# A 0/1 matrix kept in DRAM as bytes in place of bfloat16, converted by the transfer that stores it

## The chip, the cores and the metric

The kernel runs on one NeuronCore of a Trainium2 chip. The metric is device microseconds (us) of one execution, and the time of a kernel is the median over its runs. Engines are called by their short names: PE (TensorE, matrix products and transposes), DVE (VectorE), ACT (ScalarE), POOL (GpSimd, which also issues indirect transfers and converting transfers), SP (SyncE, which issues most plain transfers). 16 DMA engines move the data of all queues.

## The reference

Four graph layers with a residual are applied one after the other to `x` (8 batches, 2048 nodes, 64 features). All use one matrix `adj` of 2048 x 2048, whose entries are 0 or 1 with ones on the diagonal, dense in its first rows and columns and sparse elsewhere.

```python
# layer 0
h = jnp.maximum(_layernorm(x), 0.0); x = x + _L0_gnn_ref(h, H, adj, ...)     # hypergraph attention, adj / deg
# layer 1
h = jnp.maximum(_layernorm(x), 0.0); x = x + _L1_gnn_ref(h, adj, ...)        # Chebyshev terms of adj
# layer 2: three steps of message passing
h = jnp.maximum(_layernorm(x), 0.0); v = h with node 0 set
for _ in range(3):
    effects = einsum('nm,bmd->bnd', adj, v)
    v = relu(concat([v, effects]) @ W1.T + b1) @ W2.T + b2
x = x + v
# layer 3: attention over adj (diagonal set to 1)
h = jnp.maximum(_layernorm(x), 0.0)
e = leaky_relu(e_src[:, :, None] + e_dst[:, None, :], 0.2)
x = x + softmax(adj * e) @ (h @ weight) + bias
```

In layer 3 a node needs, one by one, only the nodes that it is linked to. So the kernel wants for each node a short list of its neighbours' numbers.

## The kernel before

Nodes are cut into 16 blocks of 128 (`P`), features into 4 groups `q` of 128 rows that hold two batches each. The program checks the data first and then branches (`tile_gnn_stack_kernel`): with sparse 0/1 data it runs `layer0_pairs`, `layer1_near`, `layer2_near` and `layer3_near`; otherwise dense versions of them. The engines meet at the branch, so the start stage ends as a whole. The trace is of the sparse branch. Each stage writes its loops in Python; a scheduler in the build puts the instructions into a fixed order on each engine, and inserts the waits. An engine runs its instructions in that order.

**The start stage** (`start`, `check_adj`). For each of the 16 blocks t, SP loads 128 rows of `adj` as float32 (1 MB, L371) into one of four row buffers. ACT squares them into bfloat16 (`squares`, four buffers, L372) and sums the degree; DVE compares row and square (L373), which proves that all entries are 0 or 1; POOL clears the diagonal (L376) and stores the squared rows into the DRAM tensor `links` (L380). PE multiplies the block with a vector of ones to find the empty tiles (`seen`). Between these, the same stage normalises `x` in four chunks of 512 nodes and makes the first features: PE, ACT and DVE share their order with that work. DVE writes the flag for the branch at its end (L639).

**Layer 2** (`layer2_near`). Three steps go over the 16 blocks. In a step, an object `Feed` brings the rows of the last step's messages from the DRAM tensor `sent`, for block 0 by plain transfers of SP (L2576), for the others by indirect gathers of POOL (L2578); six `raw` buffers are in flight. ACT rounds each raw tile (`part_hi`, L2595), DVE makes the remainder (`part_lo`, L2596), PE adds both products into the accumulator `acc`. DVE adds a block's own term and writes the finished tile `z` (L2639), PE transposes it (`pz`, L1918), ACT applies the relu (L1920), PE forms the next message `pn`, DVE adds a constant and writes `u` (L1872), which SP stores to `sent` (L1876). Up to two blocks are late behind the one that is gathered.

**The neighbour lists** (`neighbours`) are made beside steps 0 and 1 of layer 2: the generator is advanced by one piece after each group of gathered tiles, and step 2 opens with what is left of it. It ranks the nodes by degree (`order`); then, for each of the blocks 1 to 15 of that order, POOL gathers the 128 rows of `links` (L1999), DVE multiplies them with the line 1, 2, 3, ... in float16 (L2003), so that a row holds the numbers of its neighbours, and takes the eight largest (L2009) as often as the block's longest list needs, erasing them in between (L2012). The list lands in `near` (L2016), which layer 3 uses. The rows lie in two buffers, the products in two others; both are views of the slot `q4` of 16 KB per partition:

```python
words = slots.tile([P, 2, N], F, name="near_rows", tag="q4")
rows = words[:, 0].bitcast(BF).rearrange("p (i n) -> p i n", i=2)
named = words[:, 1].bitcast(F16).rearrange("p (i n) -> p i n", i=2)
```

The trace calls the slots `q`, so L2003 appears there as `q<-q,q`.

Of the kernel before, what the change touches and what calls it, by code (L numbers as in the profile page):

```python
# [8 lines left out]
BF = mybir.dt.bfloat16  # L9
# [12 lines left out]
N = 2048  # L22
# [31 lines left out]
class Slots:  # L54
# [3 lines left out]
    def __init__(self, pool):  # L58
        self.flat = {f"q{i}": pool.tile([P, 2 * N], F, name=f"q{i}") for i in range(6)}
        self.pool = None  # L60
# [74 lines left out]
class Kernel:  # L135
# [8 lines left out]
    def __init__(self, tc, ctx, a):  # L144
        self.tc, self.nc, self.a = tc, tc.nc, a
        self.flip = 0
        self.short = False
        self.consts = ctx.enter_context(tc.tile_pool(reuse_waits="tile", name="consts", bufs=1))

        dram = ctx.enter_context(tc.tile_pool(reuse_waits="tile", name="dram", bufs=1, space=bass.MemoryType.DRAM))  # L150
        self.xs = [
            [a["xT"][:, :, c * CW : (c + 1) * CW].rearrange("q p n -> p q n") for c in range(NC)]
        ]


        self.h_rows = dram.tile([N, ROW], F, name="h_rows")
        self.g_rows = dram.tile([N, NB * D], F, name="g_rows")
        self.order3 = dram.tile([P, 2, NT], I32, name="order3")

        self.links = dram.tile([N, N], BF, name="links")  # L160
        self.sent = [dram.tile([N, NB * D], F, name=f"sent{i}") for i in range(5)]


        self.f_rows = dram.tile([N, WIDE], F, name="f_rows")
        self.att_rows = dram.tile([N, NB * D], F, name="att_rows")
        self.rdeg = dram.tile([NT, P], F, name="rdeg")

        self.h_sums = [dram.tile([8, P, CW], F, name=f"sums{q}") for q in range(NP)]
        self.h_parts = [dram.tile([P, 3, N], BF, name=f"parts{q}") for q in range(NP)]
        for i in range(3):  # L170
            self.xs.append([dram.tile([P, NP, CW], F, name=f"x{i}_{c}") for c in range(NC)])
        self.setup()
# [1802 lines left out]
    def neighbours(self, k, bank, slots):  # L1975

        nc = self.nc
        order = k.tile([P, 2, NT], I32, name="order")  # L1980
        w = Parts(slots.tile([P, 2 * N], F, name="sort", tag="q4"))
        rank = self.ranks(w, bank, 1, NEAR[1])
        yield
        self.by_rank(w, bank, rank, order)
        nc.sync.dma_start(self.order3, order)
        yield
        near = self.near
        words = slots.tile([P, 2, N], F, name="near_rows", tag="q4")
        rows = words[:, 0].bitcast(BF).rearrange("p (i n) -> p i n", i=2)
        named = words[:, 1].bitcast(F16).rearrange("p (i n) -> p i n", i=2)  # L1990
        words = slots.tile([P, 2, N], F, name="line", tag="q5")
        whole = words[:, 0].bitcast(I32)
        line = words[:, 1, : N // 2].bitcast(F16)
        nc.gpsimd.iota(whole, pattern=[[1, N]], base=1, channel_multiplier=0)
        nc.vector.tensor_copy(line, whole)
        yield
        for t in range(1, NT):
            raw, row = rows[:, t % 2], named[:, t % 2]
            nc.gpsimd.indirect_dma_start(  # L1999
                raw, None, self.links[:],  # L2000
                bass.IndirectOffsetOnAxis(ap=order[:, 1, t : t + 1], axis=0),
            )
            nc.vector.tensor_mul(row, raw, line)  # L2003
            yield
            most = -(-NEAR[t] // 8)
            top = k.tile([P, 24], F, name="top", bufs=2)
            for i in range(most):
                eight = top[:, 8 * i : 8 * i + 8]
                nc.vector.max(out=eight, in_=row)  # L2009
                yield  # L2010
                if i + 1 < most:
                    nc.vector.match_replace(  # L2012
                        out=row, in_to_replace=eight, in_values=row, imm_value=0.0
                    )
                    yield
            nc.vector.tensor_copy(near[:, FIRST[t] : FIRST[t + 1]], top[:, : NEAR[t]])  # L2016
# [1113 lines left out]
```

## Time and profile before

| | |
|---|---|
| median of 4 runs | 2032.41 us (2028.54 to 2039.38) |
| the profiled execution | 2035.78 us, its span 2034.0 us |
| mean granted clock of PE | 0.902 of full speed |
| busy shares of the span | PE 84%, DVE 69%, POOL 51%, ACT 40% |
| DMA, mean over the span | 305.20 MB, 150 GB/s |
| L380, stores of `links` | 16 of 512 KB, issued from 20.5 to 90.9 us |
| L1999, gathers of `links` | 15, issued from 1326.2 to 1536.8 us |
| L2003, multiplications | 15, 1217 ns mean |

A span is the time between the first and the last instruction that the profiler sees; the execution's own time has a little around it. All places below are in us from the start of the span. A line of a timeline gives start, duration, engine, line of the kernel, instruction, what it writes and reads; in square brackets stands how long the engine was idle before it and what ended that. A wait line gives the total, how often, and the longest.

### The profile page before, as it was taken

Reading aid. Unit: us, or ns where it says so; the run is one execution under the profiler, and the core shown is the slowest. Engines: PE = TensorE matmul, PEld = TensorE weight load, DVE = VectorE, ACT = ScalarE, POOL = GpSimd, SP = SyncE. Lnnn points to the kernel's source line nnn. Section 1 sums busy time; section 2 is a strip of 40 time slices with the busy share of each in tenths; the row PEclk is TensorE's granted clock in tenths of the full one; section 3 lists DMA queues with packets and bytes.
Section 4 is the critical chain, followed back from the end, with each engine's and each line's share of the span. In section 5 each row is a group of like instructions: output and inputs, shape, how many; then the busy total and the mean of one; then the engine's idle time right before and its main releaser. Section 6 shows DMA issues by size and latency. Waiting matters only on the chain. (4 is left out here: it accounts for less than half of the span.)

```text
span 2034.0 us, 22332 instructions
## 1 busy us (share of the span) xinstructions
PE 1717.2 (84%) x7061; PEld 977.8 (48%) x7066; DVE 1411.4 (69%) x2389; ACT 808.7 (40%) x1627; POOL 1038.7 (51%) x959
## 2 busy tenths in 40 slices
PE   6859899999896778999999998779788898578885
PEld 2425766665224444443443343557566564334432
DVE  6778778884576666776767556688787566357874
ACT  5712344554555653222110100455556553166400
POOL 1100166676861644876655545364564531557870
PEclk8867899998887888999999999789899899678997
DMA  9640223334326774232230211577677664746655
GB/s 345 245 117 1 82 77 102 110 125 162 118 73 206 227 243 141 78 100 82 71 91 25 83 51 43 180 216 253 215 237 254 203 209 151 243 137 172 174 171 190
DMA packets 124057, 305.20 MB, mean 150 GB/s; under 512 B 29312, under 2 KB 31120, under 8 KB 118160
## 3 DMA queue, kind: packets, MB, share of 16 engines
q0 software_dynamic: 45328, 149.60, 24.2%
q1 hardware_dynamic: 76288, 149.80, 21.9%
q10 hardware_dynamic: 2304, 4.20, 0.6%
q8 instruction: 59, 0.97, 0.2%
q14 instruction: 78, 0.64, 0.1%
HBM read 240.40 MB, written 63.14 MB: 149 GB/s over the span
## 5 line engine op out<-in xcount | busy, mean ns | idle before, releaser
L2578 POOL DMA_INDIRECT raw<-sent,index x300 | 316.8, 1056 | 339.4 <-DVE part_lo L2596 139.8
L2596 DVE TENSOR_TENSOR part_lo<-raw,part_hi 128x512 fp32r<-128x512 f32 x352 | 265.2, 777 | 134.0 <-ACT part_hi L2595 83.2
L2595 ACT CAST part_hi<-raw 128x512 fp32r<-128x512 f32 x352 | 210.8, 619 | 312.2 <-PE acc L176 223.5
L1840 POOL TENSOR_TENSOR half<-half,y 128x512 f32<-128x512 f32 x192 | 247.1, 1316 | 134.2 <-DVE y L1834 129.0
L176 PE MATMUL pk<-q,w 128*128 128x512 f32 (+1 forms) x768 | 302.0, 610 | 2.3 <-DVE q L1724 0.9
L176 PE MATMUL acc<-q,ident 128*128 128x512 f32 x416 | 206.0, 619 | 42.8 <-issue 23.8
L176 PE MATMUL acc<-part_hi,weights 128*128 128x512 f32 x365 | 176.4, 486 | 31.6 <-ACT part_hi L2595 21.3
L176 PE MATMUL acc<-part_lo,weights 128*128 128x512 f32 x365 | 169.4, 466 | 38.0 <-DVE part_lo L2596 25.2
L1834 DVE SCALAR_TENSOR_TENSOR y<-pk,bias,q 128x512 f32<-128x512 f32 x224 | 158.0, 743 | 52.1 <-PE pk L176 32.9
L176 PEld LDWEIGHTS pk<-q,w 128*128 128x128 f32 (+1 forms) x768 | 116.0, 190 | 156.2 <-issue 120.9
L2819 POOL DMA_INDIRECT ring<-f_rows,near x121 | 142.2, 1176 | 71.8 <-issue 31.3
L176 PEld LDWEIGHTS acc<-q,ident 128*128 128x128 f32 x416 | 77.1, 196 | 120.8 <-issue 74.1
L176 PEld LDWEIGHTS acc<-part_lo,weights 128*128 128x128 f32 x365 | 74.5, 204 | 92.1 <-DVE part_lo L2596 50.9
L2305 POOL TENSOR_TENSOR q<-q,beta 128x512 f32<-128x512 f32 x57 | 76.0, 1336 | 72.5 <-DVE beta L2281 33.8
L176 PEld LDWEIGHTS acc<-part_hi,weights 128*128 128x128 f32 x365 | 74.4, 204 | 78.9 <-issue 41.2
L176 PE MATMUL pp<-adj,x_ind_hi 128*128 128x512 f32 x256 | 89.4, 465 | 0.5 <-DVE q L846 0.3
L2890 DVE TENSOR_TENSOR q<-ring,e 128x1024 f32<-128x1024 f32 x58 | 70.0, 1218 | 22.1 <-remote 17.3
L2564 ACT CAST hub_weights<-dense 128x384 fp32r<-128x384 bf16 x80 | 40.6, 512 | 109.2 <-PE acc L176 101.6
L2305 POOL TENSOR_TENSOR q<-q,coef 128x512 f32<-128x512 f32 x57 | 63.0, 1106 | 21.0 <-DVE q L2328 17.6
L176 PE MATMUL pp<-adj,x_ind_lo 128*128 128x512 f32 x256 | 72.7, 403 | 0.0
L287 DVE RECIPROCAL std<-std 128x512 f32<-128x512 f32 x16 | 53.6, 3351 | 26.8 <-ACT std L286 26.8
L2489 POOL DMA_INDIRECT listed_raw<-in_adjT_dram,cell x60 | 63.2, 1053 | 16.5 <-issue 16.1
(503 smaller groups left out, 3443.7 us busy)
## 6 DMA issues: line engine op xcount, KB each, us to landing
rows<-in_adj_dram SPq DMA_DIRECT2D x16, 1024.0 KB
adj_t<-in_adjT_dram SPq DMA_DIRECT2D x64, 256.0 KB
own<-sent SPq DMA_DIRECT2D x52, 256.0 KB
raw<-sent SPq DMA_DIRECT2D x52, 256.0 KB
sent<-u SPq DMA_DIRECT2D x48, 256.0 KB
q<-x SPq DMA_DIRECT2D x10, 1024.0 KB
x<-q SPq DMA_DIRECT2D x9, 1024.0 KB
links<-squares POOLq DMA_DIRECT2D x16, 512.0 KB
```

Of the source, the lines that this page charges most:

```text
L176: self.nc.tensor.matmul(out, lhsT, rhs, start=start, stop=stop)
L287: nc.vector.reciprocal(std, std)
L1834: nc.vector.scalar_tensor_tensor(y, pks[b, half], bias[:, b : b + 1], emb[:, b], op0=OP.add, op1=OP.mult,)
L1840: add.tensor_add(acc, acc, y)
L2305: self.nc.gpsimd.tensor_tensor(x, x, by.unsqueeze(2).to_broadcast([P, NB, D]), op=OP.mult)
L2489: self.kern.behind(nc.gpsimd.indirect_dma_start(raw[:, i], None, rows, bass.IndirectOffsetOnAxis(ap=self.cell[:, c + i : c + i + 1], axis= ...
L2564: self.nc.scalar.copy(to, self.lists.dense[:, :, i * P : (i + 1) * P])
L2578: self.nc.gpsimd.indirect_dma_start(raw, None, self.rows[:], bass.IndirectOffsetOnAxis(ap=self.lists.index[:, c : c + 1], axis=0),)
L2595: nc.scalar.copy(hi, raw)
L2596: nc.vector.tensor_sub(lo, raw, hi.bitcast(F))
L2819: self.nc.gpsimd.indirect_dma_start(to, None, self.kern.f_rows[:], bass.IndirectOffsetOnAxis(ap=index, axis=0))
L2890: nc.vector.tensor_tensor(y.rearrange("n i (b f) -> n i b f", b=NB), block[:, i : i + 2, : NB * D].rearrange("n i (b f) -> n i b f", b=NB) ...
```

## The change

`links` becomes a tensor of unsigned bytes. The store at L380 reads bfloat16 from SBUF and writes bytes, so the transfer converts; its text is the same as before. A gather at L1999 brings 2 KB per row in place of 4 KB, into the lower half of the old place; the multiplication at L2003 reads bytes and a float16 line, and writes float16 as before.

```diff
-        self.links = dram.tile([N, N], BF, name="links")
+        self.links = dram.tile([N, N], mybir.dt.uint8, name="links")
...
-        rows = words[:, 0].bitcast(BF).rearrange("p (i n) -> p i n", i=2)
+        rows = words[:, 0, : N // 2].bitcast(mybir.dt.uint8).rearrange("p (i n) -> p i n", i=2)
```

The scheduler gives the same order as before outside layer 2. Within it, some instructions trade places with near neighbours on PE, ACT, DVE, POOL and SP.

## The prediction

> **What bounds the kernel now.** I first asked where the links are touched: the groups and the instructions of the tile links. There are two places: 16 stores (L380, 20.5 to 90.9 us) and 15 gathers (L1999, 1326 to 1537 us) with a multiplication behind each (L2003). I then read each place in its own stage, since the chain that ended last begins only at 1597 us. The busy times by stretch, for layer 2 while the rows are sorted into lists (after the length of a stretch come PE, PEld, DVE, ACT and POOL busy with their instructions, then granted clock, DMA share, GB/s):
>
> ```profile
> core 0: us, PE busy (x) PEld busy (x) DVE busy (x) ACT busy (x) POOL busy (x), PEclk, DMA share, GB/s
> 1330.00:1440.00 110.00, 91.44 (x489) 71.68 (x490) 100.25 (x124) 61.82 (x124) 56.80 (x51) 0.91 0.75 237
> 1440.00:1478.00 38.00, 27.39 (x114) 20.22 (x113) 23.48 (x30) 20.11 (x40) 26.42 (x25) 0.82 0.66 204
> 1478.00:1560.00 82.00, 71.63 (x422) 60.40 (x423) 69.54 (x95) 45.43 (x95) 41.89 (x40) 0.96 0.80 256
> ```
>
> DVE is busy for 91% of the first stretch and is the limit; in the second it has 14.5 us of slack; in the third PE (87%) and DVE (85%) wait for each other. The DVE groups of 1320 to 1560 us (busy, mean ns, then idle time before):
>
> ```profile
> L2009 DVE MAX8 top<-q 128x8 f32<-128x2048 f16 x21 | 48.0, 2286 | 0.0
> L2003 DVE TENSOR_TENSOR q<-q,q 128x2048 f16<-128x2048 bf16 x15 | 18.3, 1217 | 0.0
> ```
>
> Both read 2048 elements per partition. L2003, whose three operands are all of 16 bits, takes little over half as long as MAX8. In the start stage, the three-operand row over 2048 elements with float32 among its inputs is as slow as MAX8:
>
> ```profile
> L373 DVE SCALAR_TENSOR_TENSOR equal<-rows,squares 128x2048 bf16<-128x2048 f32 x16 | 36.7, 2293 | 5.0 <-ACT squares L372 4.8
> ```
>
> Next, DVE in order of time, to see what stands behind a multiplication:
>
> ```profile
> 1397.53 1.88 DVE L2596 TENSOR_TENSOR part_lo<-raw,part_hi 128x512 fp32r<-128x512 f32 x3
> 1399.34 0.17 DVE L2016 COPY near<-top 128x12 f32<-128x12 f32 x1
> 1399.43 1.21 DVE L2003 TENSOR_TENSOR q<-q,q 128x2048 f16<-128x2048 bf16 x1
> 1400.56 0.73 DVE L2639 SCALAR_TENSOR_TENSOR z<-own,self_weight,acc 128x512 f32<-128x512 f32 x1
> ```
>
> z, the finished tile of the step, starts the moment L2003 is done. PE transposes it at 1401.65 (L1918), 0.36 us after z is ready at 1401.29. So L2003 has 0.36 us to spare here.
>
> The start stage is the other place. Between 10 and 80 us the DMA engines are 98% busy. What of that reaches the path is read from ACT's waits of 10 to 100 us, and from ACT in order of time:
>
> ```profile
> ACT squares L372 <- DMA rows<-in_adj_dram: 8.7, 3, 5.1
> ACT squares L372 <- POOL squares L376: 2.0, 2, 1.7
> ```
>
> ```profile
> 43.38 1.91 ACT L372 ACTIVATE squares<-rows 128x2048 bf16<-128x2048 f32 x1 [5.13 <-DMA rows<-in_adj_dram]
> ```
>
> One wait is large: row block 6 arrives 5.13 us late, and ACT's copies for the layer normalisation stand behind it. The queues of 10 to 100 us (packets, MB, share of 16 engines):
>
> ```profile
> q1 hardware_dynamic: 6886, 19.41, 59.3%
> q0 software_dynamic: 2304, 8.39, 23.0%
> ```
>
> **The change part by part.**
>
> *The multiplication, L2003.* Its first operand becomes bytes. No row here shows an operand of 8 bits. Bounds: 1.22 us (nothing lost) and 2.29 us (the rows of 2048 elements at one element per step). I take 2.29: the only rows near 1.2 us for two sources have all operands of 16 bits. That is +1.07 us, 15 times, 16.0 us of DVE. The Trainium skill, "VectorE: DVE Perf Modes", section "What auto-detection actually checks", says that two elements per cycle from packing need every tensor of the instruction to be 16-bit; its table for 2048 elements gives about 1224 and 2293 ns for two speeds and one, and the first agrees with the 1217 ns measured here. By that rule the bytes cost what I took from MAX8; by the hopeful end of the rows they would cost nothing.
>
> How much of the 16.0 us reaches the end I work out for each multiplication:
> - Five at 1331 to 1421 us, in the stretch that DVE limits. Behind the first DVE has no idle time until the second. For the other four the spare time between the end of the z behind them and its transposition on PE is 0 (PE had already waited 2.84 us for z), 0.05, 0.36 and 0.22 us. Delay: 5 x 1.07 - 0.63 = 4.7 us.
> - Three at 1440, 1455 and 1467 us. The next idle times of DVE behind them are 2.06, 3.89 and 2.17 us, and POOL issues its gathers there nearly back to back. Cover: those idle times, which end with data from POOL's gathers or from ACT. If it failed, because a later part_lo frees POOL's buffers later, it would cost 3.2 us. I take 1.0.
> - Seven at 1478 to 1553 us. z is transposed 0.06, 0.06, 0.23, 0.06, 0.27, 0.89 and 0.59 us after its end; the start costs of PE make the 0.06 nothing to spare. Delay: 7 x 1.07 - 0.23 - 0.27 - 0.89 - 0.59 = 5.5 us.
>
> Together 11.2 us, with ends of 0 (all of it swallowed by other waits of PE) and 16.0. Behind L2003 on DVE are queued z, u and the part_lo of the next tile; PE waits for z and part_lo, POOL's gathers for the buffers that part_lo frees. Steps 0 and 1 pass the delay on whole: step 2 opens only when all lists are done.
>
> *The 15 gathers, L1999.* POOL still issues 15 instructions of 0.94 us for 128 rows each; each row is 2 KB in place of 4 KB, so 3.9 of the 36.2 MB of the software queue between 1320 and 1560 us go. ACT's part_hi waits 13.7 us for raw gathers from that queue; 11% of it is 1.5 us, and not all lies on the path. I take -1.0 us, ends 0 and -3.
>
> *The 16 stores, L380.* The issue on POOL is 0.55 us and POOL is idle for 71 us before its affine selects; a dearer issue is covered by that. The transfer reads 4 KB per partition as before and writes 2 KB. 23.0% of 90 us is 20.7 us with all 16 engines, 1.3 us a store. No transfer here converts. Bounds from this row: priced by the bytes written, it halves; with the conversion as a second pass, it doubles. Four stores (blocks 0 to 3) are issued before the late block 6 lands, 5.2 us of engine time: -2.6 us or +5.2 us at that wait. Over all 16 stores it is -10.3 or +20.7 us of engine time, of which the hopeful side finds only the 8.7 + 2.0 us of waits above, and the DVE order (57 of 70 us busy) behind them. I take 0, the middle of two bounds without a row to choose by, because the side that is read keeps its rows of 4 KB and the engines' time is what is full; the queues ran at 23 and 25 GB/s an engine while they were (19.41 MB in 59.3%, 8.39 MB in 23.0%, of 16 engines for 90 us). The Trainium skill, "DMA: Bandwidth & Descriptors", section "Anatomy of one DMA", prices a transfer at about 2.0 us plus its bytes over 436 GB/s, and does not say which side's bytes count when the two differ; by the written side its estimate is 0.6 us less a store.
>
> *Order.* The order of the instructions differs only in layer 2: one gather of links is issued one raw gather earlier, one multiplication stands before a u and not behind it, a few sent stores trade places with raw loads on SP's queue, and on PE the hub products and part products interleave differently. Nothing crosses a step. I price it at 0, ends -3 and +3, about half of the time from one z to the next (z starts at 1384.0, 1391.0, 1396.3 and 1400.6 us). No buffer and no wait is added.
>
> **Sum.** 4.7 + 1.0 + 5.5 - 1.0 + 0 + 0 = +10.2 us. The profiled execution took 2035.78 us (span 2034.0); with the change it would be 2046.0. It lies 3.4 us above the median of the runs, 2032.41, so the median becomes 2042.6 us. The likeliest case's own range, with 5 to 16.0 us for L2003 and the rest as above, is 2036 to 2047.
>
> **The rivals.**
>
> *The conversion is dear.* If a store keeps its engines twice as long, block 6 comes 5.2 us later, blocks 8 to 11 find four more stores ahead, and ACT's reuse of the four squares buffers, which already waits for the store of block 7 (issued 51.8 us, free at 61.4), waits for longer. Some 10 to 20 us on top of layer 2: 2053 to 2063. For it: DMA 98% busy for 70 us, and stores are a quarter of it. Against it: the packets read stay the same.
>
> *Not slower: layer 2 swallows the multiplications.* In the third stretch PE is idle for 10.4 us and ACT waits 18.5 us for PE. If the delayed z only eats idle time that PE has anyway, less than 4 us of the 11.2 stay; with 1.5 us from the gathers and 2.6 us at block 6 the total is about zero: 2030 to 2036. It decides if the z behind L2003 is late by less than the next wait of PE for something else, tile by tile. Against it: 91% DVE in the first stretch, whose 4.7 us have nowhere to go.
>
> *The bytes don't slow DVE.* L2003 stays at 1.22 us; -1 us from the gathers is left: about 2031.
>
> **How the numbers follow.** Forecast 0.54, half of it on each side of +0.5% (2042.6); dear conversion 0.22; swallowed 0.18; bytes free 0.06. 0.5% or 10 us is about what a measurement of this kernel can tell from no change; the four runs span 2028.5 to 2039.4. Slower by more: 0.27 + 0.21 = 0.48. Within: 0.27 + 0.20 of the other three = 0.47. Faster: 0.05, where a cheaper store lets the whole start stage shrink. The range reaches down to 2031, which holds the swallowed case but for its lower part, and up to 2057, which holds the lower part of the dear one.
>
> **What would show it.** L2003 at about 2290 ns; DVE busy up by 16 us in 1330 to 1560 and the end of step 1 (last L2003 at 1552.6) later by 10 us than the start of that stage; the z to pz spare times gone. The start: flag (L639), at 106.4 us now, within 2 us. I am wrong if L2003 stays at 1.2 us, if flag moves by over 5 us, or if q0's share in 10 to 100 us leaves 23% by more than a quarter.

## The result, and the profile after

| | before | after |
|---|---|---|
| median | 2034.97 us (78 runs, 2022.99 to 2050.15) | 2037.38 us (52 runs, 2025.05 to 2053.76) |
| ratio, 95% interval | | 1.0016 [1.0004, 1.0029] |

The change costs 3.3 us by the ratio (0.8 to 5.9): less than the bound of 0.5% and a third of the +10.2 us of the sum. On another chip, in the first experiment, the same kernel stood at 0.9983 [0.9964, 1.0001]. The two intervals just don't meet, so the cost isn't the same on every chip, or is known less well than one interval says.

The lines of after come from an execution of 2029.89 us (span 2028.1) of the first experiment, on a chip where the kernel before takes 2025.46 us, because the first profiled one (2061.30 us) lies above all 52 timed ones, with most of its surplus behind layer 2. The nodes are ranked (L539) 6 us earlier in it than in the profile of before, so the three stretches are moved by 6 us (columns as before):

```profile
core 0: us, PE busy (x) PEld busy (x) DVE busy (x) ACT busy (x) POOL busy (x), PEclk, DMA share, GB/s
1324.00:1434.00 110.00, 90.21 (x483) 69.73 (x484) 102.90 (x122) 61.92 (x124) 59.65 (x53) 0.92 0.73 224
1434.00:1472.00 38.00, 28.37 (x119) 21.29 (x118) 28.52 (x33) 20.93 (x41) 27.22 (x24) 0.78 0.61 178
1472.00:1554.00 82.00, 72.72 (x405) 59.19 (x405) 74.74 (x89) 47.45 (x95) 49.63 (x42) 0.92 0.75 233
```

DVE has 2.6, 5.0 and 5.2 us more in the three. PE's busy time hardly moves (191.3 in all, 190.5 before), and POOL's grows by 11.4 us, which no part of the sum had. The DVE groups of layer 2:

```profile
L2009 DVE MAX8 top<-q 128x8 f32<-128x2048 f16 x21 | 48.0, 2287 | 0.0
L2003 DVE TENSOR_TENSOR q<-q,q 128x2048 f16<-128x2048 uint8 x15 | 34.3, 2287 | 0.0
```

The multiplication runs at the speed of MAX8: 34.3 us in place of 18.3, the 16.0 us of the sum.

The multiplication that had 0.36 us to spare, in order of time over all engines (in brackets the idle time before, and what ended it):

```profile
1395.43 1.29 DVE L2596 TENSOR_TENSOR part_lo<-raw,part_hi 128x512 fp32r<-128x512 f32 x2
...
1396.64 0.18 DVE L2016 COPY near<-top 128x12 f32<-128x12 f32 x1
...
1396.73 2.28 DVE L2003 TENSOR_TENSOR q<-q,q 128x2048 f16<-128x2048 uint8 x1
...
1398.93 0.73 DVE L2639 SCALAR_TENSOR_TENSOR z<-own,self_weight,acc 128x512 f32<-128x512 f32 x1
...
1399.72 0.42 PEld L1918 LDWEIGHTS pz<-ident,z 128*128 128x128 f32 x4 [0.56 <-DVE z L2639]
```

This tile is as the forecast saw it: of the 1.07 us, the spare 0.36 are gone, and PE's weight load now waits 0.56 us for z. The question is why fifteen such delays don't add up to 11 us.

In the start, ACT's waits of 10 to 100 us, its late block 6, and the queues (packets, MB, share of 16 engines):

```profile
ACT squares L372 <- DMA rows<-in_adj_dram: 9.3, 4, 4.7
...
ACT squares L372 <- DMA links<-squares: 2.0, 2, 1.2
```

```profile
43.12 1.91 ACT L372 ACTIVATE squares<-rows 128x2048 bf16<-128x2048 f32 x1 [4.74 <-DMA rows<-in_adj_dram]
```

```profile
q1 hardware_dynamic: 6922, 19.41, 60.2%
q0 software_dynamic: 2304, 4.20, 25.1%
```

Half the bytes are written, in as many packets, and the engines are held a little longer, not shorter: 25.1% against 23.0%. Block 6 is 4.74 us late (5.13 before), and the flag (L639) comes at 107.8 us (106.4).

### The profile page after: what moved, and what is told of

It reads as the page before. It is cut to its first block, busy times and chain, and to the rows that moved or that the text cites. A ratio compares the mean times of both kernels' runs of the same rounds, so it can differ in the third digit from the quotient of the medians.

```text
span 2059.5 us, 22328 instructions
## 1 busy us (share of the span) xinstructions
PE 1730.2 (84%) x7061; PEld 983.7 (48%) x7066; DVE 1425.1 (69%) x2389; ACT 810.0 (39%) x1627; POOL 1048.9 (51%) x959
## 3 DMA queue, kind: packets, MB, share of 16 engines
q0 software_dynamic: 44368, 141.47, 23.7%
## 4 chain that ended last, share of the span: by engine, by line
PE 47%; DVE 13%; issue 9%; DMA 7%; POOL 6%; ACT 2%; another core or an unknown queue 2%; SPq 0%; POOLq 0%; DVEq 0%; ACTq 0%
PE pk L176 18%; PE acc L176 16%; POOL q L2305 3%; PE bank L176 3%; DMA raw<-sent,index 2%; PE p L176 2%; POOL raw L2578 1%; DVE q L2320 1%; PE pd L176 1%; DVE part_lo L2596 1%; PE pz L1918 1%; PE pn L176 1%; POOL ring L2819 1%; PE first L176 1%
## 5 line engine op out<-in xcount | busy, mean ns | idle before, releaser
L2578 POOL DMA_INDIRECT raw<-sent,index x300 | 329.9, 1100 | 334.0 <-DVE part_lo L2596 128.1
L176 PE MATMUL acc<-q,ident 128*128 128x512 f32 x416 | 214.0, 640 | 48.4 <-issue 20.1
L2890 DVE TENSOR_TENSOR q<-ring,e 128x1024 f32<-128x1024 f32 x58 | 69.9, 1217 | 26.3 <-remote 14.6
```

What stands on the lines that cost most here:

```text
L176: self.nc.tensor.matmul(out, lhsT, rhs, start=start, stop=stop)
L2578: self.nc.gpsimd.indirect_dma_start(raw, None, self.rows[:], bass.IndirectOffsetOnAxis(ap=self.lists.index[:, c : c + 1], axis=0),)
L2890: nc.vector.tensor_tensor(y.rearrange("n i (b f) -> n i b f", b=NB), block[:, i : i + 2, : NB * D].rearrange("n i (b f) -> n i b f", b=NB) ...
```

## The experiments

Besides the times I use one stretch of each profile: **steps 0 and 1 of layer 2**, from the order of the nodes (L539) to the end of the last z of step 1. It took 230.2 us before and 233.8 us in the profile shown above (236.2 in the first one of after). A single execution scatters by some 7 us to either side as a whole, so one such number is weak by itself.

### Which half costs: one part of the change at a time

These ran beside one another on one chip (before: 2025.46 us). **Again**, the changed kernel as it is:

> The changed kernel once more, for a second profile. Theory A (the multiplication's 16 us of DVE reach the end in part, the converting stores cost nothing): about 3 us over before, flag (L639) within 1 us of 106.4, and the last multiplication (L2003) 3 to 6 us later relative to flag. Theory B (DVE's time is swallowed altogether, the converting stores lengthen the start): flag 1.5 to 3 us later, the distance from flag to the last L2003 unchanged. The first profile had flag at 108.1 us and the last L2003 at 1557.8, against 106.4 and 1552.6 of before.

Measured: 2023.54 us, ratio 0.9983 [0.9964, 1.0001]; steps 0 and 1 in 233.8 us.

**16-bit integers**: the store converts as in the change, but nothing gets smaller and the multiplication keeps 16-bit operands. In the gathered rows, `BF` becomes `uint16` too.

```diff
-        self.links = dram.tile([N, N], BF, name="links")
+        self.links = dram.tile([N, N], mybir.dt.uint16, name="links")
```

> links kept as 16-bit unsigned integers: the store still converts, but every transfer has the bytes of before, and all operands of L2003 have 16 bits. Order as before on all engines. Theory A: L2003 stays at 1217 ns, time within 2 us of before. Theory B: 2 to 4 us slower, all of it before flag. q0 between 10 and 100 us: 23% if converting costs the engines nothing, 25% or more if it does.

Measured: 2030.19 us, 1.0007 [0.9978, 1.0037]; 232.1 us.

**A float32 line**: the kernel before with only L2003 slow.

```diff
-        line = words[:, 1, : N // 2].bitcast(F16)
+        line = words[:, 1]
```

> before, with the line of numbers in float32: plain stores and gathers of bfloat16, and only L2003 slow (2290 ns instead of 1217). By the sum of the prediction 11.2 us slower (4.7 + 1.0 + 5.5). Theory A as the result of the change suggests: 3 to 6 us. Theory B: 0 to 1 us. Flag unchanged in all.

Measured: 2028.69 us, 1.0024 [0.9991, 1.0058]; 234.9 us.

**The gather converts back**: bytes in DRAM, but bfloat16 rows in SBUF, so that the multiplication is the old one.

```diff
-        rows = words[:, 0, : N // 2].bitcast(mybir.dt.uint8).rearrange("p (i n) -> p i n", i=2)
+        rows = words[:, 0].bitcast(BF).rearrange("p (i n) -> p i n", i=2)
```

> links as bytes, stored by the converting transfer, and converted back to bfloat16 by the gather (L1999), so that L2003 reads bfloat16 at 1217 ns. Order as before. Theory A: no slower than before, up to 2 us faster, as the gathers read half the bytes. Theory B: slower by what the start loses, 2 to 3 us. If converting in the gather is dear, the first L2003 waits for its gather and L1999 issues take over 0.95 us on POOL.

Measured: 2032.44 us, 1.0040 [1.0012, 1.0069]; 232.2 us. The multiplication with 16-bit integers, then with the float32 line (a line names the type of the first operand alone):

```profile
L2003 DVE TENSOR_TENSOR q<-q,q x15: 1209/1217/1220, 1323.0 to 1540.3; 128x2048 f16<-128x2048 uint16 x15
```

```profile
L2003 DVE TENSOR_TENSOR q<-q,q x15: 2274/2282/2315, 1328.7 to 1547.9; 128x2048 f16<-128x2048 bf16 x15
```

The queue of the stores, q0, from 10 to 100 us, with 16-bit integers, float32 line and converting gather:

```profile
q0 software_dynamic: 2304, 8.39, 25.5%
```

```profile
q0 software_dynamic: 2304, 8.39, 23.7%
```

```profile
q0 software_dynamic: 2304, 4.20, 25.4%
```

The same queue over steps 0 and 1, with the changed kernel's gathers (2 KB a row on both sides) and with the converting ones (2 KB read, 4 KB written):

```profile
q0 software_dynamic: 9834, 32.23, 47.9%
```

```profile
q0 software_dynamic: 10760, 36.03, 51.3%
```

What follows. The first two lines say that the width of the operands decides (min/median/max in ns): integers of 16 bits keep 1217 ns, one 32-bit operand among two of 16 bits takes it away. The next three say that a store that converts holds its engines for 25.4 to 25.5% whether it writes 8.39 or 4.20 MB, and one that doesn't for 23.7% (23.0 before): the bytes written don't price it, and the conversion adds about a tenth. What all these stores have in common is the bytes read and the number of packets, and these runs don't part the two. The last two lines say that the side that is read isn't the price of every transfer: the converting gather reads half the bytes and holds the engines for 119.1 us (51.3% of 232.2), about as long as the plain one of 4 KB (120.7 with 16-bit integers), the gather of 2 KB for 112.0. The larger side, or the packets, would fit all of them. The flag came at 107.0, 107.7 and 107.0 us, the middle one without any conversion: nothing of the conversion is seen at the end of the start. By time, only the changed kernel run again and the converting gather have intervals that don't meet (0.9983 and 1.0040); the others can't be ranked. The converting gather isn't faster than before, so this route back to 16 bits is no gain; why its interval lies above 1 isn't shown by its stages (232.2 us, flag 107.0).

### Was it the order, or the slow multiplication?

A slow multiplication also makes the scheduler give another order, on PE above all in how hub products and part products interleave. From here the theories are those of the texts that follow: A, the delay falls into waits that were there; B, the new order hides it. The wish was a slow multiplication under the old order, or a fast one under the new; three edits of the kernel before were made for that.

```diff
-        line = words[:, 1, : N // 2].bitcast(F16)
+        line = words[:, 1].bitcast(F16)[:, 1 : N + 1]
```

> The kernel before, with the line 1, 2, 3, ... of L2003 one element (2 bytes) further on in its place. The order of the instructions on every engine is that of the kernel before. Should the multiplication be slow on the chip with a line at an odd place (near 2290 ns), this is the slow multiplication under the old order. Measure: from the order's store (L539) to the end of the last z (L2639) of step 1, which was 230.2, 232.1 and 232.2 us in the three kernels with a fast multiplication and 236.2, 233.8 and 234.9 in the three with a slow one. Theory A (slow multiplications fall mostly into time in which DVE and PE would have waited for each other in any case): 234 to 236 us under the old order too. Theory B (the new order of the scheduler, which puts hub products between part products on PE, fills the gaps; under the old one the delay would count in full as forecast): 240 to 246 us. Should L2003 stay at 1217 ns, it is one more sample of the kernel before (231.5 us), and tells neither apart.

Measured: L2003 1217 ns; 2025.76 us, 0.9997 [0.9970, 1.0023]; 232.4 us.

```diff
-            nc.vector.tensor_mul(row, raw, line)
+            nc.vector.tensor_mul(row, raw, line[:, ::-1])
```

> The kernel before, with the line of L2003 read backwards, so that the neighbours' numbers, and with them the result of layer 3, are others. Order of the instructions as before. Should a backward read make the multiplication slow (near 2290 ns), it is a second slow multiplication under the old order: theory A 234 to 236 us for steps 0 and 1 of layer 2, theory B 240 to 246 us. Should it stay at 1217 ns, about 231.5 us, and it tells nothing of the two.

Measured: L2003 1217 ns; 2029.23 us, 1.0008 [0.9975, 1.0041]; 232.8 us.

```diff
-        line = words[:, 1, : N // 2].bitcast(F16)
+        line = words[:, 1].bitcast(F16).rearrange("p (n i) -> p n i", i=2)[:, 0]
```

> The kernel before, with the 16-bit line of L2003 laid at every second element. The scheduler takes the multiplication for a slow one and gives the order that it gives with a float32 line (nearly that of the changed kernel). Should the multiplication be fast on the chip (near 1217 ns), this is the fast multiplication under the new order: theory A 230 to 232.5 us for steps 0 and 1 (the order is worth nothing by itself), theory B 222 to 227 us (the order gives what the slowness takes). Should it be slow (near 2290 ns), it repeats the float32 line, 234 to 236 us by both, and says that a step of two costs a 16-bit operand its speed.

Measured: L2003 2282 ns; 2028.16 us, 0.9995 [0.9961, 1.0028]; 239.8 us. So all three missed what they were for: the first two are further samples of the kernel before, the third one of the float32 line. What they give is a better mean. Five profiles with the multiplication at 1217 ns under the old order (230.2, 232.1, 232.2, 232.4, 232.8) have 231.9 us, four with it at 2282 to 2287 ns (236.2, 233.8, 234.9, 239.8) have 236.2 us: **4.2 us of the 16**, with a scatter of 1.0 among the five and of 2.6 among the four, so that the 4.2 are known to some 3 us. By parts, means of the five and of the four: from the order to the last z of step 0 101.8 and 104.4 us (+2.6), from there to the first z of step 1 56.5 and 54.5 (-2.0), and through step 1 73.6 and 77.3 (+3.7).

PE's waits over steps 0 and 1 (total, how often, longest; the odd line, fast, then the changed kernel):

```profile
PE acc L176 <- DVE part_lo L2596: 17.2, 11, 2.1
PE pz L1918 <- DVE z L2639: 6.1, 6, 2.8
```

```profile
PE acc L176 <- DVE part_lo L2596: 11.1, 8, 2.1
PE pz L1918 <- DVE z L2639: 8.2, 8, 2.2
```

PE waits 2.1 us more for z, and 6.1 us less for part_lo. The delay is there, but PE stops for something else less often. That fits A and B alike. Two things limit this reading. For 9.0 and 10.9 us of PE's waits the two traces name no cause ("issue"). And PE's idle time as a whole fell from 43.4 to 39.4 us, while its busy time rose from 189.0 to 194.4: on these chips the longer stretch isn't made of waits of PE that the trace shows, and why the same products were busy for longer stays open (the traces hold 1009 and 1022 records of them).

### When does DVE decide? The dose doubled

```diff
             nc.vector.tensor_mul(row, raw, line)
+            nc.vector.tensor_mul(row, raw, line)
```

> The changed kernel with every multiplication of L2003 made twice (30 of about 2285 ns in place of 15, with an order of the scheduler's own): 34 us more work of DVE beside steps 0 and 1 than in the changed kernel, 50 us more than before. Theory A (a fifth of the added DVE time reaches the end): steps 0 and 1 at 241 to 244 us, the time 7 to 9 us over the changed kernel's. Rival (the spare time of DVE is used up by the change's 16 us, and what comes after counts in full): 265 to 270 us, the time over 30 us longer. Third theory (DVE is never what ends layer 2): 234 to 237 us, no difference.

Measured: 2050.53 us, 1.0136 [1.0094, 1.0178] of before; steps 0 and 1 in 254.5 us.

```profile
L2003 DVE TENSOR_TENSOR q<-q,q 128x2048 f16<-128x2048 uint8 x15 | 34.2, 2283 | 0.0
L2004 DVE TENSOR_TENSOR q<-q,q 128x2048 f16<-128x2048 uint8 x15 | 34.2, 2281 | 0.0
```

Against the four slow profiles, 34.2 us more of DVE make 18.3 us (254.5 - 236.2): a half, where the first 16 us made a quarter. It is between the first two theories, and the third (DVE never decides) falls. That layer 2 had some slack for DVE on these chips, which the change used up, would fit; it isn't shown, since the scheduler gave this kernel too an order of its own.

### The dose taken away

The multiplications move to the start, where the store then writes the numbers themselves:

```diff
+            nc.vector.tensor_mul(named[:, t % 2], sq, line)
-            nc.gpsimd.dma_start(self.links[here], sq)
+            nc.gpsimd.dma_start(self.links[here], named[:, t % 2])
...
-            raw, row = rows[:, t % 2], named[:, t % 2]
+            raw = row = rows[:, t % ROWS]
...
-            nc.vector.tensor_mul(row, raw, line)
```

`links` is float16 here, and `ROWS` is 4. It ran on a chip where the kernel before takes 1980.45 us.

> The kernel before with the multiplications moved out of layer 2: at the start DVE multiplies each block's squares with the line 1, 2, 3, ... (16 multiplications, 1.22 us each by the kernel before) and the plain 16-bit store writes the numbers themselves; in layer 2 the gathers bring finished rows into four buffers, and L2003 is gone: 15 x 1.217 = 18.3 us less of DVE beside steps 0 and 1 (before: 231.9 us on the mean of five kernels with a fast multiplication). Theory A (most of DVE's time there lies beside waits of DVE and PE for each other, and the less of it there is the less each us counts: 0.27 us per us for the change's 16): 227 to 231 us for steps 0 and 1. Theory B (every us of DVE there counts as in the forecast, 0.7): 218 to 221 us. Theory C (nothing is to be had below the kernel before, the waits being for other things): 231 to 233 us. The start has 19.5 us more of DVE: the flag (106.3 to 108.1 us in all kernels so far) at 106 to 109 us if the loads of adj set its end, up to 120 us if DVE does.

Measured: 1979.82 us, 0.9996 [0.9973, 1.0020]. The flag:

```profile
L646 DVE TENSOR_SCALAR flag<-one x1: 142/142/142, 115.5 to 115.5; 1x1 int32<-1x1 f32 x1
```

That is 8.9 us later than the 106.6 of the other kernel that ran on that chip, whose start is the old one. The whole is -0.8 us (-5.3 to +4.0), so about 10 us (the 8.9, by one profile of each, and 0.8) were gained behind the start, and given back in it. That speaks against theory C, but the gain needn't be DVE's alone: the rows also have four buffers in place of two, and the line is made at the start. No version tried is measurably faster than before. Steps 0 and 1 took 207.5 us; the 231.9 us of the expectation are of other chips, and the one profile on that chip that comes near the old order, of the next experiment, has 227.5 us in an execution 16 us above the median of before.

### What makes a 16-bit multiplication slow

One look, with different forms of L2003 in its fifteen places, on that same chip (the kernel also clears the products' buffers once):

```diff
-            nc.vector.tensor_mul(row, raw, line)
+            if t < 5:
+                pair = lambda x: x.rearrange("p (n a) -> p n a", a=2)
+                nc.vector.tensor_mul(pair(row), pair(raw), pair(line)[:, :, ::-1])
+            elif t < 9:
+                three = lambda x: x[:, :2046].rearrange("p (n a) -> p n a", a=3)
+                nc.vector.tensor_mul(three(row), three(raw), line[:, :3].unsqueeze(1).to_broadcast([P, 682, 3]))
+            elif t < 12:
+                nc.vector.tensor_mul(row[:, 1:], raw[:, 1:], line[:, 1:])
+            else:
+                nc.vector.tensor_mul(row[:, 1:], raw[:, :-1], line[:, 1:])
```

> Only to see what makes L2003 slow while its operands stay 16-bit, as a step of two did (2282 ns) and an odd place and a backward read of the line did not (1217 ns): the multiplications of blocks 1 to 4 read the line by swapped pairs, those of blocks 5 to 8 go by runs of three elements with the line's first three repeated, blocks 9 to 11 have all operands one element further on and 2047 elements, blocks 12 to 14 and 15 the same with the gathered row at its even place. The lists, and with them layer 3, are others. If the fast form needs only a step of one in the innermost run, all stay at 1217 ns; forms that need pairs of neighbouring elements at an even place would be near 2282 ns.

Measured (min/median/max in ns):

```profile
L2006 DVE TENSOR_TENSOR q<-q,q x4: 1211/1216/1224, 1325.5 to 1396.1; 128x2048 f16<-128x2048 bf16 x4
L2009 DVE TENSOR_TENSOR q<-q,q x4: 1569/1572/1573, 1416.4 to 1459.8; 128x2046 f16<-128x2046 bf16 x4
L2011 DVE TENSOR_TENSOR q<-q,q x3: 1211/1216/1218, 1470.1 to 1496.7; 128x2047 f16<-128x2047 bf16 x3
L2013 DVE TENSOR_TENSOR q<-q,q x4: 1211/1216/1220, 1509.4 to 1540.8; 128x2047 f16<-128x2047 bf16 x4
```

Swapped pairs and odd places cost nothing; runs of three take 29% longer. It gave no slow form under the old order. Its time, 1996.18 us, is a single run and not read.

### The fast multiplication under the new order

The scheduler judges an operand by the shape it is written in, and an empty last dimension makes it take the multiplication for slow, while the instruction that is built has the plain shape:

```diff
-            nc.vector.tensor_mul(row, raw, line)
+            nc.vector.tensor_mul(row.unsqueeze(2), raw.unsqueeze(2), line.unsqueeze(2))
```

> The kernel before, with the operands of L2003 written with an empty last dimension of size 1. The scheduler takes the multiplication for a slow one, and gives instruction for instruction the order that it gives with a float32 line; the instruction itself is the plain one again, so that it should take 1217 ns: the fast multiplication under the new order, which the step of two was not. Theory A (the slow multiplication falls mostly into waits that would have been there, and the order is worth nothing by itself): steps 0 and 1 of layer 2 at 230 to 233 us, as with a fast multiplication under the old order (231.9 on the mean of five). Theory B (the order fills gaps and hides what the slowness costs): 222 to 228 us, and a time 4 to 10 us below the kernel before. Theory C (the new order is itself the loss, the slowness costs nothing): 234 to 238 us, as with a slow one.

Beside it, on the same chip (before: 1981.04 us), the float32 line with the very same order:

> The float32 line again (slow multiplication of 2282 ns, the same order as the run beside it, everything else as in the kernel before), so that both have one chip and one set of runs of before. Theory A: steps 0 and 1 at 234 to 238 us, 3 to 5 us over the run beside it, and the time 3 to 5 us over it as well. Theory B: 234 to 238 us, 8 to 12 us over the run beside it. Theory C: no difference between the two.

Measured: with 1216 ns 1978.67 us, 0.9991 [0.9975, 1.0007]; with 2281 ns 1989.82 us, 1.0043 [1.0026, 1.0061]. Steps 0 and 1, 215.1 and 230.8 us, by the windows (columns as above), and PE's waits there, of the fast one and then of the slow one:

```profile
1304.80:1519.90 215.10, 185.60 (x1015) 147.51 (x1014) 191.42 (x248) 131.68 (x263) 131.25 (x122) 0.93 0.80 258
```

```profile
1312.20:1543.00 230.80, 191.32 (x1027) 149.99 (x1025) 207.02 (x248) 131.81 (x263) 140.79 (x122) 0.92 0.77 242
```

```profile
PE acc L176 <- DVE part_lo L2596: 11.2, 11, 2.3
PE pz L1918 <- DVE z L2639: 8.5, 10, 2.8
```

```profile
PE pz L1918 <- DVE z L2639: 17.3, 15, 3.9
PE acc L176 <- DVE part_lo L2596: 11.7, 12, 2.3
```

What follows. With the order held still, the wait for part_lo stays (11.2 and 11.7 us), and the wait for z doubles: nothing is exchanged, and the slow multiplication costs 11.2 us between the medians (1989.82 - 1978.67; by the two intervals together, 0.0052 +/- 0.0024, some 6 to 15 us). The 15.7 us between the two windows, of which PE stands idle for 10.0 and is busy for 5.7, are no measure of it: the two profiled executions (1971.08 and 1997.96 us) were the fastest and the slowest of their twelve. The order by itself is worth -1.8 us (-5.0 to +1.4), so theory C falls, and B at its own figure (4 to 10 us below before) does so but for its edge, though its 8 to 12 us between the two kernels are met. A's 3 to 5 us are too few as well. The drop of the wait for part_lo between the odd line and the changed kernel goes with the order and not with the slowness: this wait is 16.8 to 21.8 us in all five profiles of a fast multiplication under the old order, 8.9 to 12.1 in the four of a slow one, and 11.2 here, where the multiplication is fast and only the order is new (20.7 in the profile of the forms above, on a chip as fast and in nearly the old order). That it fell by 6 to 11 us and the time by hardly 2 says that one sum of waits isn't time won.

## Why the prediction was right, and where its sum was off

The time, 2037.38 us, lies in the range and under 0.5% from before. Part of that is luck. The median of before is 2034.97 us in these runs, 2.6 above the 2032.41 from which the prediction started. By difference, +3.3 us lie just under the likeliest case (2036 to 2047, which is +3.6 to +14.6) and at the upper end of the swallowed rival (2030 to 2036), which had a chance of 0.18. On the way there one term was too large.

**L2003.** Taken at 2.29 us; it is 2.287. The 16.0 us of DVE are as summed.

**How much of it reaches the end: the term that was mis-sized.** The sum had 11.2 us (4.7, 1.0 and 5.5 in the three stretches). The result leaves 3.3 us in all, which with the -1.0 for the gathers is 4.3 for this term (1.8 to 6.9), and the profiles of the chips near 2030 us say 4.2. The three stretches of the sum are step 0, the time between the steps, and step 1: there the profiles show +2.6, -2.0 and +3.7 where it put 4.7, 1.0 and 5.5. What failed is the rule of its working: it set each late z against the transposition behind it and passed the delay on whole. That the delayed z eats time in which PE stood anyway was the mechanism of the second rival, which turns out to hold in part: 11 of 16 us were forecast, a quarter was paid.

But the rival isn't right either. Under one and the same order the slowness cost 11.2 us on another chip, and the interval of 6 to 15 contains the sum's 11.2. Against the old order, as the change is measured, the float32 line cost 8.5 us there (5.2 to 12.1). What lies between that and 3.3 (0.8 to 5.9) the runs don't say. It can be the chip (the stages with many transfers are longer on those of the result, and DVE's delay may have more to hide behind). It can be a saving by the smaller transfers, which the float32 line hasn't: q0 held the engines for 112.0 us in steps 0 and 1 of the changed kernel and for 115 to 121 with gathers that write 4 KB a row. It can be the order, since that of the changed kernel isn't quite that of the float32 line: in the two traces DVE, ACT and POOL do a few instructions of step 0 in another order. And part of it can be chance, since the two intervals meet and the changed kernel itself moved from +3.3 to -3.4 us (-7.3 to +0.2) on another chip. For the chip speaks that the step of two cost -1.0 us (-7.9 to +5.7) and the float32 line +4.9 (-1.8 to +11.7) on the slower chips, but both intervals reach above 5.2; for the transfers, that the changed kernel lies below the float32 line on one chip (0.9983 and 1.0024), but these intervals meet too. The converting gather says nothing against the transfers, for it saves no time of the engines. The changed kernel beside the last pair would have told; it wasn't run there.

**Gathers, -1.0 us.** Not confirmed and not refuted: the engines were held for 112.0 us in place of 115.5 and more, but no comparison of times resolves 1 us.

**Stores, 0.** Right in size: the share of q0 rose by 2.1 points of 90 us, 1.9 us of engine time over 16 stores, far from -10.3 and +20.7. The prediction's reason was that the side that is read keeps its bytes; the runs show that the bytes written don't count here, but not whether it is the bytes read or the packets, which also stayed the same. The estimate of 0.6 us less a store, by the written side, doesn't hold. The dear conversion falls.

**Order, 0 within 3.** Not contradicted: -1.8 us (-5.0 to +1.4), for the order of the float32 line, which is nearly that of the changed kernel.

**Bytes don't slow DVE.** Falls at 2287 ns.

**The signs that were named.** L2003, the flag (+1.4 us) and q0's share came as said. DVE busy rose by 12.9 us in the three stretches rather than 16, and by 15.1 us over the whole of steps 0 and 1 (207.5 in the changed kernel, 192.4 with the odd line). The end of step 1 came later by 4 us after the ranking, not 10.

## What to carry to other kernels

A narrower type in DRAM pays only if the transfers that shrink are what the stage waits for, and its price is read at the consumer: here an operand of 8 bits took from DVE the speed of two 16-bit ones, and the halved bytes bought nothing that could be measured. The delay of one instruction against its next reader isn't yet what reaches the end; ask what else that reader would have waited for, and price both. And a changed duration changes the scheduler's order too: hold the order still, as the empty dimension did, before the two are told apart.

## What the runs showed of the hardware that was not expected

**POOL's gathers stop for the multiplication.** A gather's issue takes 0.95 us, but often longer when it begins beside L2003 or part_lo, whose operands are two tiles in SBUF. The odd line (fast) and the changed kernel (slow) at the same place of the order, DVE and POOL in order of time:

```profile
1463.78 1.22 DVE L2003 TENSOR_TENSOR q<-q,q 128x2048 f16<-128x2048 bf16 x1
1464.06 1.76 POOL L2578 DMA_INDIRECT raw<-sent,index  x1 [3.06 <-DVE near L2016]
```

```profile
1462.21 2.29 DVE L2003 TENSOR_TENSOR q<-q,q 128x2048 f16<-128x2048 uint8 x1
1462.50 2.82 POOL L2578 DMA_INDIRECT raw<-sent,index  x1 [1.25 <-DVE near L2016]
```

Both gathers are done 0.82 us after their multiplication (1465.82 against 1465.00, 1465.32 against 1464.50). In the changed kernel 12 of the 13 gathers that began during an L2003 ended 0.82 or 0.83 us after it. Of those that began during a MAX8, which is as long but reads one tile, all 32 kept 0.94 or 0.95 us. So a slow multiplication holds back POOL too: the 107 gathers of L2578 had a mean of 1079 ns with the fast one and 1181 with the slow one, 10.8 us more of POOL in steps 0 and 1. With the order held still it is 9.5 us more (131.25 and 140.79 in the last pair). The prediction had no such term, and what it is worth in time the runs don't show. The Trainium skill, "SBUF — State Buffer", section "Who interferes with whom", says that a DVE instruction with two inputs in SBUF contends with a GpSimd instruction that reads SBUF; these lines agree, for a gather that reads its index there.

**Chips differ by more than the change.** The kernel before took 2025 to 2035 us on some and 1980 to 1981 us on others. Between the odd line and the fast multiplication under the new order, which differ by 55.5 us in the spans of their profiles (some 2 of them by the order), the time up to the ranking is 12.4 us longer, steps 0 and 1 17.3 (232.4 against 215.1), step 2 14.3 (153.5 against 139.2) and the rest 11.5: most of it in the stages where the DMA share is 0.59 and more, little for their length in the 1200 us before them, where it is below 0.5. What is slower there, these runs don't show.

**Where a 16-bit operand loses its speed.** An odd place (2 bytes off) and a backward read kept 1217 ns, a step of two took 2282, and runs of three 1572.
